# An RWKV attention and mixture-of-experts block on one core: the front's statistics, ramps, parameter loads and pieces in another order

## The chip, the cores and the metric

The kernel runs on one core of one Trainium2 chip. The metric is the device time of one execution in microseconds. Five engines work side by side: TensorE (PE in the profile, its weight loads PEld), VectorE (DVE), ScalarE (ACT), GpSimd (POOL) and SyncE (SP, which here only issues transfers). Each engine works through its own list of instructions in order. Transfers are issued by SP, ACT and POOL.

## The reference

x has 2 sequences of 2048 tokens and 256 channels, 4096 tokens in all. It is normalized twice for the attention branch, which projects three blends of each token with the token before it, runs a decaying sum over time and projects the result. The expert branch sends each token to the best two of eight experts.

```python
xn = _layernorm(x)
# attention branch: a second layer norm, with gain ln_g and bias ln_b
x2 = _layernorm(xn, ln_g, ln_b);  last = x2 shifted by one token (zero at the start)
k = (x2*mix_k + last*(1-mix_k)) @ Wk.T      # v and r likewise, with their own mix
den = den*td + exp(k);  num = num*td + exp(k)*v          # over time
attn = (sigmoid(r) * num/(den + 1e-8)) @ Wo.T
# expert branch, on xn
scores = relu(xn @ Wr + br);  the two best experts, softmax of their scores as weights
y_e = relu(xn @ W1[e] + b1[e]) @ W2[e] + b2[e]
out = x + attn + sum of weight_e * y_e
```

## The kernel before

The tokens are cut into 8 blocks of 512, and a block into 4 tiles of 128 tokens. The order of all instructions is written out by hand: the program's text is the order on each engine. The front, up to about 57 us, goes over the 8 blocks with small functions that the text calls in turn:

- load_x(b) loads a block, load_w() the next of wk, wv, wr and wo; the loop at L151 loads the six parameter vectors into the rows of one tile. SP issues the loads but for two tiles of x's block 0 and the six vectors, which ACT issues. In the compiled program a transfer of SP or ACT uses one of eight completion semaphores in turn, and waits until the transfer that had the same one before has landed.
- keep_warm(n) is n products on PE over a tile of zeros, idle, whose result nobody reads.
- stats(b): DVE takes mean and variance of each token (bn_stats, bn_aggr, L225 and L227), and POOL forms w from the variance (L230), its power of -1/2, rr (L233), for blocks 2 and 3 also mrr (L237), and ve (L238).
- normed(b): (x - mean) * rr for four tiles (L260), on DVE; in blocks 2 and 3 the first of the four on ACT (L264), with mrr. Then a store into the table that the experts gather from (L267).
- turned(b): PE transposes the block (L292), ACT writes it twice, as x2T (L295) and with the gain and bias as xaT (L305). In block 0 the first blend is made straight from the transposes (L297 on ACT, L301 on DVE), with first_by, which needs the parameter vectors: PE transposes these (colp, L488), ACT copies them to cols (L490), and DVE works unmixed and first_by out of them. x2T of block 0 is copied by DVE in turned_on() (L320).
- follow(b): POOL copies the last column of one block's xaT in front of the next's.
- mix(n): the next n of the 24 blends on DVE (L385); parts(b, i): what ACT prepares for them (L350).
- some(n): the next n of the 48 pieces of the projections. A piece is four products on PE (L415) and an evacuation by ACT (L418). From the tenth piece on each also lets ACT do one of parts.
- scored(b) and routed(b): the router's products (L330), a copy by ACT (L336) and a transpose (L341). When all eight are there, best_two() on DVE chooses the experts; divisors(h) on POOL is a power over 16 columns (L244) that it needs.

PSUM has two buffers for pieces and scores together (ps_a) and two for transposes (ps_t); blends have six, x2 three.

While pieces of later blocks run, DVE sorts the tokens by expert with tables of comparisons against the ramps lo_iota and hi_iota (L530). Then comes the expert stage, from 115 us to the end: for each unit of 128 or 256 tokens PE does the first product (L1000) and the second (L1013), weights are loaded by SP, tokens gathered and results added by POOL, and the decaying sum runs beside it on DVE.

The ramps, e_iota and other tables are written by POOL after stats(1). The memset of idle is DVE's last before the first statistics.

Of the kernel before, what the change touches and what calls it, by code (L numbers as in the profile page):

```python
# [9 lines left out]
F32 = mybir.dt.float32  # L10
BF16 = mybir.dt.bfloat16
F16 = mybir.dt.float16
# [14 lines left out]
def rwkv_moe_block(  # L27
# [42 lines left out]
    NU = K * NT + E - 1  # L70
# [38 lines left out]
    xa_pool = routing.enter_context(tc.tile_pool(name="xa", bufs=1))  # L109
    rout = routing.enter_context(tc.tile_pool(name="rout", bufs=1))  # L110
    fronts = routing.enter_context(ExitStack())
    rpool = fronts.enter_context(tc.tile_pool(name="rpool", bufs=2, side="right"))
# [36 lines left out]
        attn_w.append(t)  # L149

    for n, i in enumerate((4, 5, 1, 2, 3, 0)):  # L151
        nc.scalar.dma_start(
            rows[i * NC : (i + 1) * NC, :], vectors[i].rearrange("(c p) -> c p", p=P)
        )

# [10 lines left out]
    for b in range(4, NB):  # L166
# [4 lines left out]

    ident = const.tile([P, P], F32, name="ident")
    make_identity(nc, ident)
    power = rout.tile([P, HT], F32, name="power")
    nc.vector.memset(power, -0.5)

# [2 lines left out]
    nc.gpsimd.iota(  # L179
        place, [[NPAIR, 2]], base=0, channel_multiplier=1, allow_small_or_imprecise_dtypes=True  # L180
    )
    at_pair = rout.tile([P, 1], F32, name="at_pair")
    at_unit = place[:, 1:2]
    wlim = rout.tile([P, 2 * E], F32, name="wlim")
# [21 lines left out]

    sd2 = const.tile([P, NT], F32, name="sd2")
    sps = [ps_y.tile([P, HT, EW], F32, tag="py", name=f"sp{h}") for h in range(2)]
    rrs, mrrs, xaTs = [None] * NB, [None] * NB, [None] * NB

    def mk(nm, shape):
        return rpool.tile(shape, F32, bufs=1, name=nm)
# [3 lines left out]
    def stats(b):  # L216
        st, mv = mk(f"st_{b}", [P, NS, 6]), mk(f"mv_{b}", [P, NS, 2])
        mean, var = mv[:, :, 0], mv[:, :, 1]
        at = ts(b, NS)
        rrs[b] = rr_all[:, at]  # L220
        w, mrr = mk(f"w_{b}", [P, NS]), None

        for half in ((0, 1), (2, 3)) if b == 0 else (range(NS),):
            for i in half:
                nc.vector.bn_stats(st[:, i, :], xts[b][:, i, :])  # L225
            for i in half:
                nc.vector.bn_aggr(mv[:, i, :], st[:, i, :])  # L227
# [5 lines left out]
            nc.gpsimd.tensor_tensor(rrs[b][:, g], w[:, g], power[:, g], ALU.pow)  # L233
        if b not in NORMED:
            less_mean, mrr = mk(f"less_mean_{b}", [P, NS]), mk(f"mrr_{b}", [P, NS])
            nc.gpsimd.tensor_scalar(less_mean, mean, -1.0, 0.0, ALU.mult, ALU.add)
            nc.gpsimd.tensor_tensor(mrr, less_mean, rrs[b], ALU.mult)  # L237
        nc.gpsimd.tensor_scalar(ve_all[:, at], var, LN_EPS, 0.0, ALU.add, ALU.add)  # L238
        mrrs[b] = (mean, mrr)

    def divisors(half):

        at = slice(half * HT, (half + 1) * HT)
        nc.gpsimd.tensor_tensor(rs[:, at], ve_all[:, at], power, ALU.pow)  # L244
# [8 lines left out]
    def normed(b):  # L253
        xt = xts[b]
        mean, mrr = mrrs[b]
        x2 = x2s[b] = rpool.tile([P, NS, C], F32, tag="x2", bufs=3, name=f"x2_{b}")
        for t in range(NS):
            r = rrs[b][:, t : t + 1]
            if t or b in NORMED:
                nc.vector.tensor_scalar(  # L260
                    x2[:, t, :], xt[:, t, :], mean[:, t : t + 1], r, ALU.subtract, ALU.mult
                )
# [55 lines left out]
    def turned_on():  # L318
        for c in range(NC):
            nc.vector.tensor_copy(x2Ts[0][:, c, :], first_tps[c])  # L320
# [17 lines left out]
    def routed(b):  # L338
        i = b * NS % HT
        sp = sps[b * NS // HT][:, i : i + NS, :]  # L340
        nc.tensor.transpose(sp.rearrange("p t e -> p (t e)"), s8s[b], ident)  # L341
# [15 lines left out]
    def weighted(b, i):  # L357
        for _ in parts(b, i):
            pass
# [34 lines left out]
    def mix(n):  # L394
        for _ in range(n):
            next(blending)
# [29 lines left out]
    def some(n):  # L426
        for _ in range(n):
            next(projected)
# [41 lines left out]
        nc.vector.tensor_tensor(hot.rearrange("p e t -> p t e"), hot1, hot2, ALU.add)  # L470

    idle = rpool.tile([P, TB], BF16, bufs=1, name="idle")
    nc.vector.memset(idle, 0.0)
    warm = ps_h.tile([P, TB], F32, tag="ph", name="warm")

    def keep_warm(n):
        for _ in range(n):
            nc.tensor.matmul(warm, idle[:, 0:P], idle, start=True, stop=True)  # L480

    xaTs[0] = xa_pool.tile([P, NC, TB + 1], F32, name="xaT_0")
    nc.gpsimd.memset(xaTs[0][:, :, 0:1], 0.0)
    keep_warm(13)
    stats(0)
    normed(0)
# [7 lines left out]
    def vecs(i):  # L494
        return cols[:, i * NC : (i + 1) * NC]
# [22 lines left out]
    def count(nm, n, dtype=F32, base=0, step=1, chan=0, pool=rout):  # L518
        t = pool.tile([P, n], dtype, name=nm)
        nc.gpsimd.iota(  # L520
            t, [[step, n]], base=base, channel_multiplier=chan,
            allow_small_or_imprecise_dtypes=True,
        )
        return t

    CH = 8

    def ramp(nm, n):
        t = rout.tile([P, n, 2], F16, name=nm)
        nc.gpsimd.iota(  # L530
            t, [[1, n], [0, 2]], base=0, channel_multiplier=0,
            allow_small_or_imprecise_dtypes=True,
        )
        return t

    lo_iota, hi_iota = ramp("lo_iota", P), ramp("hi_iota", NU)
    e_iota = count("e_iota", E)

    token = rout.tile([P, NT], F16, name="token")
    for i in range(2):  # L540
        nc.gpsimd.iota(
            token[:, i * HT : (i + 1) * HT], [[P, HT]], base=(-NTOK // 2, 1)[i],
            channel_multiplier=1, allow_small_or_imprecise_dtypes=True,
# [5 lines left out]
        base=NTOK, channel_multiplier=1, allow_small_or_imprecise_dtypes=True,  # L549
# [3 lines left out]
        allow_small_or_imprecise_dtypes=True,  # L553
# [6 lines left out]
    keep_warm(2)  # L560
    some(2)
    mix(1)
    normed(1)
    turned_on()
    weighted(0, 2)
    some(2)
    turned(1)
    follow(1)
    nc.scalar.activation(td, vecs(0), AF.Exp)
    mix(1)  # L570
    scored(0)
    stats(2)
    some(2)
    routed(0)
    mix(1)
    normed(2)
    scored(1)
    some(1)
    turned(2)
    follow(2)  # L580
    stats(3)
    mix(1)
    normed(3)
    some(1)
    routed(1)
    some(1)
    scored(2)
    turned(3)
    follow(3)
    for i in range(2):  # L590
        nc.sync.dma_start(acc[NTOK + i * P : NTOK + (i + 1) * P, :], zero)
    stats(4)
    some(1)
    mix(1)
    normed(4)
    routed(2)
    some(1)
    scored(3)
    turned(4)
    follow(4)  # L600
    stats(5)
    some(1)
    routed(3)
    mix(1)
    normed(5)
    some(1)
    scored(4)
    turned(5)
    follow(5)
    stats(6)  # L610
    divisors(0)
    some(1)
    mix(1)
    normed(6)
    routed(4)
    some(1)
    scored(5)
    turned(6)
    follow(6)
    stats(7)  # L620
    divisors(1)
    some(1)
    mix(1)
    normed(7)
    routed(5)
    scored(6)
    turned(7)
    follow(7)
# [420 lines left out]
    for s in range(NSTEP):  # L1049
# [102 lines left out]
```

## Time and profile before

| | us |
|---|---|
| median of 3 runs (lowest, highest) | 654.92 (654.69, 655.28) |
| the profiled execution | 655.4 |
| its span, first to last instruction | 653.7 |
| PE busy | 635.7 (97%) |
| DVE busy | 334.7 (51%) |
| ACT busy | 230.4 (35%) |
| POOL busy | 242.0 (37%) |
| DVE busy from 20 to 50 us | 8.76, 8.97 and 8.69 of each 10 |
| ACT busy from 20 to 50 us | 6.84, 8.76 and 9.28 of each 10 |

A group of instructions is given as line, engine, operation, output<-input, sizes and count. What stands in brackets behind an instruction is how long its engine was idle just before it and what ended that. Products on PE are pipelined, so that the time from one start to the next tells more than a duration. In a table of waits the columns are the waiting engine, what it waits to do, and who released it; then the total in us, how many times, and the longest.

### The profile page before, as it was taken

How to read it: one execution, taken by the hardware profiler on the slowest of the kernel's cores; microseconds unless marked ns; L12 is line 12 of the kernel's file. 1: busy time of each engine (PE TensorE's matmuls, PEld its weight loads, DVE VectorE, ACT ScalarE, POOL GpSimd, SP SyncE). 2: the span in 40 equal slices, each digit the busy share in tenths (PEclk: the TensorE clock that was granted, in tenths of full speed). 3: DMA queues.
4: the chain of work that ended last, by engine and by line, in shares of the span. 5: the costliest groups of instructions: out<-in, count | busy, mean ns of one | idle time of the engine just before them, and what ended most of it. 6: DMA issues, size and time to landing. Idle time of an engine off the chain costs nothing. (4 is left out here: it accounts for less than half of the span.)

```text
span 653.7 us, 9070 instructions
## 1 busy us (share of the span) xinstructions
PE 635.7 (97%) x3030; PEld 496.5 (76%) x3030; DVE 334.7 (51%) x776; ACT 230.4 (35%) x474; POOL 242.0 (37%) x212
## 2 busy tenths in 40 slices
PE   7999999999999999999999999999999999999993
PEld 3454444888888888888888888888888888888882
DVE  6988997646546555757676857222211212221110
ACT  4696754342332333232323232322332222222220
POOL 3664204043243354304434373443443333343111
PEclk9999999999999999999999999999999999999997
DMA  8534505697796795789686777666667665667611
GB/s 244 199 125 163 146 0 148 244 295 204 184 315 188 189 314 182 198 274 313 185 199 178 199 204 202 185 190 178 182 193 214 211 212 173 172 181 202 194 22 17
DMA packets 92424, 124.50 MB, mean 190 GB/s; under 512 B 15468, under 2 KB 80568, under 8 KB 92248
## 3 DMA queue, kind: packets, MB, share of 16 engines
q1 hardware_dynamic: 74592, 100.77, 47.2%
q0 software_dynamic: 17472, 22.86, 18.9%
q8 instruction: 25, 0.41, 0.2%
q10 hardware_dynamic: 312, 0.27, 0.2%
q14 instruction: 23, 0.19, 0.1%
HBM read 105.89 MB, written 26.38 MB: 202 GB/s over the span
## 5 line engine op out<-in xcount | busy, mean ns | idle before, releaser
L1004 ACT ACTIVATE h<-hp,b 128x256 f32<-128x256 f32 (+1 forms) x296 | 136.2, 460 | 348.6 <-PE hp L1000 234.6
L1000 PE MATMUL hp<-xT,w 128*128 128x256 f32 (+1 forms) x1184 | 252.5, 369 | 0.9
L1013 PE MATMUL yp<-w,h 128*128 128x256 f32 x1104 | 244.4, 379 | 0.0
L1000 PEld LDWEIGHTS hp<-xT,w 128*128 128x128 f32 x1184 | 199.0, 189 | 49.8 <-ACT h L1004 18.8
L1013 PEld LDWEIGHTS yp<-w,h 128*128 128x128 f32 x1104 | 207.0, 190 | 26.6
L1025 POOL DMA_INDIRECT out_dram<-y,into x50 | 84.0, 1680 | 209.7 <-DVE y L1021 112.1
L990 DVE COPY xT<-xp 128x512 f32<-128x512 f32 (+1 forms) x37 | 24.3, 656 | 167.8 <-PE xp L988 167.8
L960 POOL DMA_INDIRECT xg<-table,frm x69 | 75.3, 1092 | 43.8 <-PE p L415 23.0
L1020 DVE TENSOR_TENSOR y<-yp,b 128x256 f32<-128x256 f32 x67 | 28.3, 423 | 105.1 <-PE yp L1013 105.1
L1025 POOL DMA_INDIRECT acc<-y,into x19 | 32.5, 1709 | 83.9 <-DVE y L1021 22.1
L898 DVE RECIPROCAL dn<-dn 128x512 f32<-128x512 f32 x16 | 53.6, 3353 | 0.5
L418 ACT ACTIVATE kvr<-p 128x512 f32<-128x512 f32 x48 | 28.7, 600 | 31.6 <-PE p L415 31.0
L415 PE MATMUL p<-mix,wk 128*128 128x512 f32 x64 | 29.8, 601 | 0.9 <-DVE mix L301 0.9
L415 PE MATMUL p<-mix,wv 128*128 128x512 f32 x64 | 29.7, 597 | 0.0
L415 PE MATMUL p<-mix,wr 128*128 128x512 f32 x64 | 29.5, 596 | 0.0
L907 PE MATMUL op<-wo,z 128*128 128x256 f32 x128 | 28.9, 379 | 0.0
L907 PEld LDWEIGHTS op<-wo,z 128*128 128x128 f32 x128 | 24.3, 190 | 3.3
L1021 DVE TENSOR_SCALAR y<-y,gate 128x256 f32<-128x256 f32 x67 | 24.6, 367 | 2.4
L385 DVE SCALAR_TENSOR_TENSOR mix<-xaT,cols,mix 128x512 f32<-128x512 f32 x34 | 24.6, 776 | 0.5 <-ACT mix L350 0.5
L350 ACT ACTIVATE mix<-xaT,unmixed 128x512 f32<-128x512 f32 x34 | 24.2, 717 | 0.0
L970 DVE TENSOR_SCALAR xg<-xg 128x256 f32<-128x256 f32 x69 | 22.7, 367 | 0.0
L415 PEld LDWEIGHTS p<-mix,wk 128*128 128x128 f32 x64 | 11.4, 190 | 13.0 <-issue 8.7
(188 smaller groups left out, 387.7 us busy)
## 6 DMA issues: line engine op xcount, KB each, us to landing
w<-in_L_ffn_W_dram SPq DMA_DIRECT2D x74, 1024.0 KB, 9.2
b<-in_L_ffn_b_dram SPq DMA_DIRECT2D x37, 128.0 KB, 4.0
table<-x SPq DMA_DIRECT2D x8, 512.0 KB, 2.9
x<-in_L_attn_x_dram SPq DMA_DIRECT2D x7, 512.0 KB, 5.8
out_dram<-o_sb POOLq DMA_DIRECT2D x5, 512.0 KB, 7.9
acc<-o_sb POOLq DMA_DIRECT2D x3, 512.0 KB, 6.2
xg<-table,frm POOLq DMA_INDIRECT x69, 6.8
out_dram<-y,into POOLq DMA_INDIRECT x50, 7.3
```

Of the source, the lines that this page charges most:

```text
L385: nc.vector.scalar_tensor_tensor(m[:, c, :], by[:, c, :], vec(1 + i, c), other[:, c, :], ALU.mult, ALU.add,)
L415: nc.tensor.matmul(p, w[:, c, ts(o, P)], m[:, c, :], start=(c == 0), stop=(c == NC - 1))
L418: nc.scalar.activation(kvr[b][:, i, o, :], p, f, scale=sign)
L898: nc.vector.reciprocal(dn, dn)
L907: nc.tensor.matmul(op, z[:, c, ts(t, P)], wo_sb[:, c, :], start=(c == 0), stop=(c == NC - 1))
L960: nc.gpsimd.indirect_dma_start(out=g, out_offset=None, in_=table, in_offset=bass.IndirectOffsetOnAxis(ap=frm[:, u : u + 1], axis=0), bound ...
L1000: nc.tensor.matmul(hp, w1_sb[:, c, ts(j, P)], xT[:, c, :], start=(c == 0), stop=(c == NC - 1))
L1004: nc.scalar.activation(h[:, 0:n], hp, AF.Relu, bias=b1_sb[:, j : j + 1])
L1013: nc.tensor.matmul(yp, hs[j][:, ts(i, P)], w2_sb[:, j, :], start=(j == 0), stop=(j == NH - 1))
L1020: nc.vector.tensor_tensor(y, yp, b2_sb, ALU.add)
L1021: nc.vector.tensor_scalar(y, y, gates[s][i], None, ALU.mult)
L1025: return nc.gpsimd.indirect_dma_start(out=to, out_offset=bass.IndirectOffsetOnAxis(ap=into[:, u : u + 1], axis=0), in_=y, in_offset=None, ...
```

## The change

- The parameter vectors: the first three (gain, bias, mix_k) are still issued by ACT, the other three (mix_v, mix_r, time_decay) by SP, behind x's block 0 and in front of wk.
- The memset of idle moves from the end of DVE's memsets to behind the first of them. The memset of xaT's first column goes in front of the ramp place on POOL.
- lo_iota and hi_iota move from behind stats(1) to POOL's very beginning, before stats(0). e_iota stays; a helper with one use left is written out.
- turned_on() now stands ahead of normed(1).
- stats(b) moves up from block 2 on: stats(2) comes directly behind turned(1), and each stats(b+1) is called before normed(b). divisors follow stats(6) and stats(7) as before.
- Pieces, blends, scores and transposes are called in another order: from block 2 on a turned comes directly behind the score of the block before it, and two pieces follow, where before one stood on each side.

The changed kernel has the same operations as before; only their order, and the queue of three small transfers, differ.

```diff
     for n, i in enumerate((4, 5, 1, 2, 3, 0)):
-        nc.scalar.dma_start(
+        (nc.scalar if n < 3 else nc.sync).dma_start(
             rows[i * NC : (i + 1) * NC, :], vectors[i].rearrange("(c p) -> c p", p=P)
         )
...
     ident = const.tile([P, P], F32, name="ident")
     make_identity(nc, ident)
+
+    idle = rpool.tile([P, TB], BF16, bufs=1, name="idle")
+    nc.vector.memset(idle, 0.0)
+    xaTs = [None] * NB
+    xaTs[0] = xa_pool.tile([P, NC, TB + 1], F32, name="xaT_0")
+    nc.gpsimd.memset(xaTs[0][:, :, 0:1], 0.0)
     power = rout.tile([P, HT], F32, name="power")
     nc.vector.memset(power, -0.5)
...
+    CH = 8
+
+    def ramp(nm, n):
+        t = rout.tile([P, n, 2], F16, name=nm)
+        nc.gpsimd.iota(
+            t, [[1, n], [0, 2]], base=0, channel_multiplier=0,
+            allow_small_or_imprecise_dtypes=True,
+        )
+        return t
+
+    lo_iota, hi_iota = ramp("lo_iota", P), ramp("hi_iota", NU)
...
-    idle = rpool.tile([P, TB], BF16, bufs=1, name="idle")
-    nc.vector.memset(idle, 0.0)
     warm = ps_h.tile([P, TB], F32, tag="ph", name="warm")
...
-    xaTs[0] = xa_pool.tile([P, NC, TB + 1], F32, name="xaT_0")
-    nc.gpsimd.memset(xaTs[0][:, :, 0:1], 0.0)
     keep_warm(13)
     stats(0)
     normed(0)
...
-    lo_iota, hi_iota = ramp("lo_iota", P), ramp("hi_iota", NU)
-    e_iota = count("e_iota", E)
+    e_iota = rout.tile([P, E], F32, name="e_iota")
+    nc.gpsimd.iota(
+        e_iota, [[1, E]], base=0, channel_multiplier=0, allow_small_or_imprecise_dtypes=True
+    )
...
     keep_warm(2)
     some(2)
     mix(1)
+    turned_on()
     normed(1)
-    turned_on()
     weighted(0, 2)
     some(2)
     turned(1)
     follow(1)
     nc.scalar.activation(td, vecs(0), AF.Exp)
+    stats(2)
     mix(1)
     scored(0)
-    stats(2)
     some(2)
     routed(0)
-    mix(1)
+    stats(3)
     normed(2)
     scored(1)
-    some(1)
+    mix(1)
     turned(2)
     follow(2)
-    stats(3)
+    some(1)
+    stats(4)
+    normed(3)
+    some(1)
+    routed(1)
     mix(1)
-    normed(3)
-    some(1)
-    routed(1)
-    some(1)
     scored(2)
     turned(3)
     follow(3)
+    some(1)
+    stats(5)
...
-    stats(6)
-    divisors(0)
-    some(1)
-    mix(1)
+    some(1)
+    stats(7)
+    some(1)
+    divisors(1)
     normed(6)
     routed(4)
-    some(1)
+    mix(1)
     scored(5)
     turned(6)
     follow(6)
-    stats(7)
-    divisors(1)
-    some(1)
-    mix(1)
+    some(1)
     normed(7)
     routed(5)
+    some(1)
+    mix(1)
     scored(6)
     turned(7)
     follow(7)
```

More of the change, by code (lines that the diff above doesn't have):

```diff
@@ L208, in rwkv_moe_block @@
     sps = [ps_y.tile([P, HT, EW], F32, tag="py", name=f"sp{h}") for h in range(2)]
-    rrs, mrrs, xaTs = [None] * NB, [None] * NB, [None] * NB
+    rrs, mrrs = [None] * NB, [None] * NB
     def mk(nm, shape):
@@ L517, in rwkv_moe_block @@
     )
[L518 to L534, printed above, removed]
-    lo_iota, hi_iota = ramp("lo_iota", P), ramp("hi_iota", NU)
-    e_iota = count("e_iota", E)
+    e_iota = rout.tile([P, E], F32, name="e_iota")
+    nc.gpsimd.iota(
+        e_iota, [[1, E]], base=0, channel_multiplier=0, allow_small_or_imprecise_dtypes=True
+    )
     token = rout.tile([P, NT], F16, name="token")
@@ L589, in rwkv_moe_block @@
     follow(3)
+    some(1)
+    stats(5)
     for i in range(2):
         nc.sync.dma_start(acc[NTOK + i * P : NTOK + (i + 1) * P, :], zero)
-    stats(4)
     some(1)
-    mix(1)
     normed(4)
     routed(2)
-    some(1)
+    mix(1)
     scored(3)
@@ L600, in rwkv_moe_block @@
     follow(4)
-    stats(5)
     some(1)
+    stats(6)
+    divisors(0)
+    some(1)
+    normed(5)
     routed(3)
     mix(1)
-    normed(5)
-    some(1)
     scored(4)
@@ L609, in rwkv_moe_block @@
     follow(5)
-    stats(6)
-    divisors(0)
     some(1)
-    mix(1)
+    stats(7)
+    some(1)
+    divisors(1)
     normed(6)
     routed(4)
-    some(1)
+    mix(1)
     scored(5)
@@ L619, in rwkv_moe_block @@
     follow(6)
-    stats(7)
-    divisors(1)
+    some(1)
+    normed(7)
+    routed(5)
     some(1)
     mix(1)
-    normed(7)
-    routed(5)
     scored(6)
```

## The prediction

> **What bounds the kernel now.** I read, in this order, the page's shares and slices, the timeline of TensorE (PE), the waits of VectorE (DVE) and of PE in the first 60 us, and the timelines of DVE, GpSimd (POOL), ScalarE (ACT) and SP there. PE is busy for 97% of the span, and its expert stage hardly waits: the line group of L1000 has 0.9 us of idle time in all. The chain of waits breaks off at the last scatter, so I follow PE itself. All edits act before about 57 us; what they give is how much earlier PE gets through this front.
>
> ```profile
> span 653.7 us, 9070 instructions
> PE 635.7 (97%) x3030; PEld 496.5 (76%) x3030; DVE 334.7 (51%) x776; ACT 230.4 (35%) x474; POOL 242.0 (37%) x212
> ```
> ```profile
> 2.68 5.73 PE L480 MATMUL warm<-idle 128*128 128x512 bf16 x13 [2.68 <-DVE idle L475]
> 8.34 0.23 PE L488 MATMUL colp<-ident,rows 12*128 12x12 f32 x1
> ...
> 10.91 3.70 PE L415 MATMUL p<-mix,wk 128*128 128x512 f32 x8 [0.89 <-DVE mix L301]
> 14.45 3.60 PE L415 MATMUL p<-mix,wv 128*128 128x512 f32 x8
> 18.65 1.22 PE L292 MATMUL tp<-ident,x 128*128 128x128 f32 x8 [0.61 <-DVE x2T L320]
> ...
> 50.22 0.64 PE L330 MATMUL p<-x2T,wr_sb 128*32 128x128 f32 x16
> 51.35 1.64 PE L292 MATMUL tp<-ident,x 128*128 128x128 f32 x8 [0.49 <-DVE x L260]
> 52.83 1.88 PE L415 MATMUL p<-mix,wr 128*128 128x512 f32 x4
> ...
> 55.84 0.33 PE L341 MATMUL sp<-ident,s 128*128 128x128 f32 x1 [0.44 <-ACT s L336]
> ...
> 57.82 0.27 PE L635 MATMUL b1p<-ident,b_rows 64*128 64x64 f32 x1
> ```
> Columns: start, duration, engine. From start to next start a piece (four products) costs 1.72 us, a block's transposes 0.93, a score 0.57, a routing 0.11. From 10.91 to 57.82 PE does 18 pieces, 7 transposes, 8 scores, 8 routings: 30.96 + 6.51 + 4.56 + 0.88 = 42.9 us of work in 46.9. So 4.0 us are lost, about 1.0 of it in 0.1 us steps when PE changes from one kind to another.
>
> ```profile
> DVE x L260 <- POOL rr_all L233: 5.8, 8, 1.2
> ```
> ```profile
> 15.34 2.57 DVE L260 TENSOR_SCALAR x<-x,mv,rr_all 128x256 f32<-128x256 f32 x4 [0.93 <-POOL rr_all L233]
> 17.83 1.27 DVE L320 COPY x2T<-tp 128x512 f32<-128x512 f32 x2
> ...
> 45.33 1.39 DVE L260 TENSOR_SCALAR x<-x,mv,rr_all 128x256 f32<-128x256 f32 x4 [0.92 <-POOL rr_all L233]
> ```
> ```profile
> 16.24 1.52 POOL L530 IOTA lo_iota<- 128x256 f16 x1
> 17.73 0.88 POOL L530 IOTA hi_iota<- 128x142 f16 x1
> ...
> 45.58 2.95 POOL L244 TENSOR_TENSOR rs<-ve_all,power 128x16 f32<-128x16 f32 x1
> ```
> DVE stands still eight times before the normalization, waiting for POOL's power of the variance. Once the four L260 take 2.57 instead of 1.39 us: the fourth starts at 16.34 and takes 1.57, until lo_iota is over.
>
> **The change, part by part.** Durations are those of the one profiled execution: span 653.7, with 1.7 around it 655.4, 0.5 over the median of 654.92. Differences found in it are taken off the median.
>
> *Warm-up.* The memset of idle moves in front of the other 13 on DVE: done at about 1.2 instead of 2.62, so warm starts at 1.25 instead of 2.68. Its 13 products follow each other by 0.427 us (5.55), so they end at 6.8 instead of 8.2. The memsets behind it end as before; DVE's wait for x until 3.82 (1.2 us) covers them.
>
> *Parameter rows.* ACT issues three (0.54, 0.24, 0.24), SP the other three, ahead of wk. In the compiled order each transfer waits until the eighth before it has landed. The last row now goes out when x's first tile has landed, by 3.82, not at 4.54. The trace has no landing time for rows: at most 3.8 us (from 4.54 to colp's weight load at 8.33), and in the nearest row, x's first tiles on this queue, 3.1. So colp can run between 6.9 and 7.6. Shorter than 3.1 gains nothing, as warm ends at 6.8. From colp to ACT's first L297 (8.34 to 9.29) are 0.95 us. L297 also needs normed(0), on DVE until 7.71 as before, its transposes, and 0.5 us of small DVE operations behind it: 8.15 at the earliest. So L297 starts between 8.15 and 8.55 and gains 1.14 to 0.74; I take 1.0, nearer the row of the same queue. The first piece starts at 9.9.
>
> *What the rows delay.* wk waits for x's fourth tile, x_1 for its third, landed by 4.44: they go out at about 4.3 and 4.7, not 1.76 and 2.24. wk took 4.9 us to land (x_2 waited for it until 6.64), so 9.2 against 9.9 where it is needed. x_1 took 5.8, at most 6.2 for any block: 10.9 against 10.44, where DVE first reads it; a 512 KB write into table took 2.9, which gives 7.6. I take zero: PE needs mix1_0 only 0.67 us after DVE has it and mix2_0 0.42 after, so up to 0.4 us late is free; beyond that it costs one for one. Later blocks are read 5 us or more after they land.
>
> *Ramps.* lo_iota and hi_iota (2.4 us) run on POOL from 1.64 to 4.1, where it sat idle until 4.88 for DVE's mv: nothing, with 0.7 to spare, then one for one on normed(0). They leave 16.24.
>
> *Block 1.* turned_on's two copies (1.19) now fill the 0.93 wait ahead of normed(1), and L260 is not held. DVE: bn and aggregates 10.44 to 12.03, mix 13.33, copies 14.52, normed(1) 15.82; before that was 19.02 with the copies. PE's transposes no longer wait: from 14.45 to 19.80 it took 5.35, it needs 3.44 + 0.93 + 0.1, which gives 0.88. stats(2) now stands before mix2_0, whose first half is there at 18.15, PE wanting it at 18.57.
>
> *Statistics a block ahead.* POOL's chain for the next block (0.6 + 1.41 and 0.55) runs beside another block's normalization, and the 5.8 us of waits go. On PE this removes what they caused: 1.13 and 1.48 from 50.22 to 52.83 instead of 0.57 and 0.93 (1.11), and the piece at 29.29, behind ACT's wait for mrr, 2.07 instead of 1.72 (0.35). In return the next block's statistics (1.60) stand before each normed on DVE: normed(2) ends at 21.3, 1.6 before PE can turn it, normed(7) near 43, six before. If that cover went, it would be one for one on turned.
>
> *Pieces dealt anew.* turned(2) follows scored(1) directly, one piece sooner, and a new wait appears: its first quarter is ACT's L264, queued behind the evacuation of wr's second piece. PE ends wr at 22.1, routes and scores until 22.88; ACT evacuates 22.3 to 22.8 and has L264 at 23.4. Behind L264 wait x2T and xaT of block 2, with PE. Bounds 0 (were L264 earlier) and 0.7 (were it queued for the whole 0.6 and 0.1); I take 0.58. From block 3 to block 6 both orders pace 5.15 us per block (0.93 + 2 × 1.72 + 0.11 + 0.57 + 0.1). The wait of routed(7) for s (0.5) stays.
>
> Sum: 1.0 + 0.88 + 1.11 + 0.35 − 0.58 = 2.76, call it 2.7. routed(7) ends near 53.5. What is late next? From 57.82 PE does six pieces until the count of the experts at 68.42; its input hot was ready at 64.45, and moves 3.2 earlier as DVE no longer works up to 56.81: covered. From 68.84 to 98.99 DVE is the bound, started by this count, so all moves together; the weight loads follow DVE's choice of experts. 654.92 − 2.7 = 652.2.
>
> **Rivals.**
> (a) *The front does not start earlier.* The rows still land with the old end of warm-up, or PE's clock opens later. The 13 warm products run at 0.427, the two at 9.42 at about half that. With warm ending at 6.8 PE idles 0.8 us, and the clock may stay slow into the first pieces. The gain is then 1.7: 653.2. The Trainium skill (TensorE: Matmul & The Clock Gate, section "Part 1: The HAM clock gate") says that a free-running window of 3.4 us has to be busy; by that rule the release could slip to about 11.5 and cost an estimated 0.8; the trace's 13 slow products agree, the phase of the window is not shown.
> (b) *New waits eat the reorder*: ACT, busy 9.3 of 10 us from 40 to 50, is late again at each turned. With only the front and 0.2 left the gain is 1.2: 653.7. Against it: ACT's work for a block is 2.26 + 0.15 + 1.0 + 1.22 = 4.6 of 5.15.
> (c) *Slower: POOL's power holds DVE.* normed(b) now runs beside the power of block b+1 (1.0 to 1.41 us), as the fourth L260 was held by lo_iota. Six normed would be held: 6.0 to 8.5 us. DVE's own work from 9.1 is 39.9 us, so it ends at 49.0, 4.2 before the score needs it at 53.2; the rest, 1.8 to 4.3, comes off the gain: 653.1 to 656.5. It is slower than before from 1.15 us per block. For it: lo_iota. Against it: the power of 45.58 took 2.95 us, and L260 beside it took its usual 1.39. The Trainium skill (SBUF — State Buffer, section "Who interferes with whom") speaks for this rival: a VectorE tensor_scalar and a GpSimd instruction share a port pair, and the second blocks until the first ends. lo_iota agrees with it, the power at 45.58 does not, and I go by the latter.
> (d) *Nothing arrives at the end*: a transfer that doesn't move sets the expert stage. 654.9. Against it: PE's 0.9 us there.
> (e) *x_1 lands later than 6.2 us after its issue.* At 8 us 1.8 is lost: 654.0.
>
> **How the numbers follow.** As worked out 0.62; (a) 0.16; (b) 0.09; (c) 0.06; (d) 0.03; (e) 0.04. Predicted 652.2. The bounds of the terms give 651.5 to 652.9 for it, with another 0.2 below for run and profile. Up to 653.7 (a) and most of (b) are in; what is left out is some 0.15. About 0.2%, 1.3 us, is what a measurement can tell from no change. Faster by more: 0.62 + 0.16 + half of (b) + 0.01 = 0.83. Slower by more: 0.05, from (c) above all and a long (e). The rest, 0.12, is within.
>
> **What would show it.** In the profile after: warm starting near 1.25, colp by 7.6, the first piece near 9.9; lo_iota over by 4.2; no wait of DVE for rr_all behind block 0; L260 at 1.3 to 1.4 for four beside every power; a PE wait of about 0.6 ahead of turned(2); b1p near 55.1 and the count near 65.7. It would be wrong if the first piece stays near 10.9, if a product waits for a transfer of wk or x, if normed takes over 2 us, or if the expert stage shows waits for weights.

## The result

| | before | after |
|---|---|---|
| median, same chip (lowest, highest) | 655.28 (654.69, 656.31), 5 runs | 651.80 (651.56, 651.85), 5 runs |
| the profiled execution, its span | 655.4, 653.7 | 651.85, 650.1 |
| first piece of the projections on PE | 10.91 | 9.65 |
| b1p, a transposition of the experts' biases: the end of the front | 57.82 | 54.81 |
| first product of the expert stage | 114.87 | 111.87 |
| from there to the end of the span | 538.8 | 538.2 |

The changed kernel takes 0.9945 of the time before, with a 95% interval of 0.993 to 0.996. It is faster by 3.5 us between the medians, against a forecast of 2.7 from 654.92, the median of the first three of the five runs before; 652.2 was forecast, 651.80 came. The last four lines of the table, from one profiled execution of each kernel, say where it is from: 1.26 us up to the first piece, 1.75 between the first piece and b1p, nothing between b1p and the first product (57.05 and 57.06), and 0.6 behind that.

The page of the changed kernel, its span and its shares:

```profile
span 650.1 us, 9068 instructions
PE 634.3 (98%) x3030; PEld 496.6 (76%) x3030; DVE 333.2 (51%) x776; ACT 230.2 (35%) x474; POOL 238.1 (37%) x212
```

PE is busy for 1.4 us less than before (634.3 for 635.7), in a span 3.6 shorter: 2.2 of the 3.6 is idle time that went. The rest is busy time that holds short waits: the transposes of block 7 took 1.64 and take 1.09, the first products of the expert stage together 252.5 and 251.9. The timeline of PE in the changed kernel (start, duration, engine, line; L494 is the warm-up, L432 a piece, L309 transposes, L347 a score, L358 a routing):

```profile
1.30 5.73 PE L494 MATMUL warm<-idle 128*128 128x512 bf16 x13 [1.30 <-DVE wlim L202]
6.96 0.26 PE L500 MATMUL colp<-ident,rows 12*128 12x12 f32 x1
...
9.65 3.70 PE L432 MATMUL p<-mix,wk 128*128 128x512 f32 x8 [0.84 <-DVE mix L318]
13.18 3.60 PE L432 MATMUL p<-mix,wv 128*128 128x512 f32 x8
16.62 1.04 PE L309 MATMUL tp<-ident,x 128*128 128x128 f32 x8
...
22.05 0.64 PE L347 MATMUL p<-x2T,wr_sb 128*32 128x128 f32 x16
23.18 1.09 PE L309 MATMUL tp<-ident,x 128*128 128x128 f32 x8 [0.49 <-ACT x L281]
...
48.32 0.64 PE L347 MATMUL p<-x2T,wr_sb 128*32 128x128 f32 x16
48.90 1.09 PE L309 MATMUL tp<-ident,x 128*128 128x128 f32 x8
...
52.83 0.33 PE L358 MATMUL sp<-ident,s 128*128 128x128 f32 x1 [0.44 <-ACT s L353]
...
54.81 0.27 PE L631 MATMUL b1p<-ident,b_rows 64*128 64x64 f32 x1
```

The transposes of block 1 (16.62) and of block 7 (48.90) now follow what stands before them without a wait. The transposes of block 2 (23.18) have a wait that was not there, 0.49 us for the quarter of normed(2) that ACT does; with the step from one kind of work to the next the score takes 1.13 there and not 0.57. The routing of block 7 still waits for ACT.

DVE's waits in the first 60 us of the changed kernel (who waits, for whom; total, times, longest):

```profile
DVE score L473 <- PE sp L358: 3.4, 1, 3.4
...
DVE x L277 <- POOL rr_all L250: 0.6, 2, 0.3
```

The eight waits for POOL's power, 5.8 us, have come down to the two of block 0. DVE is now early by 3.4 us at the end of the front (it waits there for the routing of block 7), where PE had waited 0.49 us for it ahead of block 7's transposes.

The ramps on POOL in the changed kernel, and on DVE the normalization of block 1, which they had held:

```profile
1.58 1.51 POOL L192 IOTA lo_iota<- 128x256 f16 x1
3.06 0.88 POOL L192 IOTA hi_iota<- 128x142 f16 x1
4.72 0.19 POOL L247 TENSOR_SCALAR w<-mv 128x2 f32<-128x2 f32 x1 [0.78 <-DVE mv L244]
```
```profile
14.26 1.54 DVE L277 TENSOR_SCALAR x<-x,mv,rr_all 128x256 f32<-128x256 f32 x4
```

They are over at 3.94, 0.78 before POOL has work, and the four normalizations take 1.54, where before they took 2.57.

### The profile page after: what moved, and what is told of

Same layout as the page of the kernel before. It is cut to its first block, busy times and chain, and to the rows that moved or that the text cites. A ratio compares the mean times of both kernels' runs of the same rounds, so it can differ in the third digit from the quotient of the medians.

```text
span 650.1 us, 9068 instructions
## 1 busy us (share of the span) xinstructions
PE 634.3 (98%) x3030; PEld 496.6 (76%) x3030; DVE 333.2 (51%) x776; ACT 230.2 (35%) x474; POOL 238.1 (37%) x212
## 5 line engine op out<-in xcount | busy, mean ns | idle before, releaser
L996 PE MATMUL hp<-xT,w 128*128 128x256 f32 (+1 forms) x1184 | 251.9, 369 | 0.8
L1021 POOL DMA_INDIRECT out_dram<-y,into x50 | 82.2, 1644 | 214.9 <-DVE y L1017 127.8
L1021 POOL DMA_INDIRECT acc<-y,into x19 | 30.6, 1608 | 85.0 <-issue 26.5
L432 PE MATMUL p<-mix,wk 128*128 128x512 f32 x64 | 29.4, 599 | 0.8 <-DVE mix L318 0.8
L432 PE MATMUL p<-mix,wv 128*128 128x512 f32 x64 | 29.5, 597 | 0.0
L432 PE MATMUL p<-mix,wr 128*128 128x512 f32 x64 | 29.5, 598 | 0.0
L432 PEld LDWEIGHTS p<-mix,wk 128*128 128x128 f32 x64 | 11.5, 190 | 13.3 <-issue 9.6
```

Source lines behind the costliest of these rows:

```text
L432: nc.tensor.matmul(p, w[:, c, ts(o, P)], m[:, c, :], start=(c == 0), stop=(c == NC - 1))
L996: nc.tensor.matmul(hp, w1_sb[:, c, ts(j, P)], xT[:, c, :], start=(c == 0), stop=(c == NC - 1))
L1021: return nc.gpsimd.indirect_dma_start(out=to, out_offset=bass.IndirectOffsetOnAxis(ap=into[:, u : u + 1], axis=0), in_=y, in_offset=None, ...
```

## The experiments

Each undoes or adds one thing; v_best and v_pre stand on v_normed. "Interior" is the time from the first piece to b1p on PE. All columns but the median are from one profiled execution. Chips differ a little, so the kernel before is given on the same chip. Its own runs spread by 1.5 us or more on each chip, so the 95% interval of a ratio reaches 0.6 to 1 us to each side: by these intervals only o_order (0.9985 to 1.0003) and v_pre (0.9902 to 0.9928) are clear of the changed kernel (0.993 to 0.996). What the other edits do is read from their traces.

| | median (before, same chip) | first piece | interior | first product | to the end |
|---|---|---|---|---|---|
| before | 655.28 | 10.91 | 46.91 | 114.87 | 538.8 |
| after | 651.80 (655.28) | 9.65 | 45.16 | 111.87 | 538.2 |
| u_warm: idle's memset last | 652.63 (655.73) | 10.91 | 45.16 | 113.12 | 538.2 |
| u_rows: six rows on ACT | 653.90 (655.73) | 11.28 | 45.17 | 113.50 | 538.9 |
| u_ramps: ramps behind stats(1) | 653.15 (655.73) | 9.65 | 46.51 | 113.20 | 538.2 |
| u_order: the old order of calls | 652.78 (655.73) | 9.61 | 45.80 | 112.45 | 538.2 |
| warm6: 6 products of warm-up | 653.41 (655.72) | 9.80 | 46.58 | 113.41 | 538.3 |
| x1_late: x_1 behind all weights | 653.05 (655.72) | 9.79 | 46.82 | 113.64 | 538.3 |
| v_normed: no quarter on ACT | 651.93 (655.72) | 9.86 | 44.73 | 111.60 | 538.8 |
| v_best: and a piece moved | 651.99 (655.72) | 9.70 | 44.55 | 111.52 | 538.8 |
| rows_behind: rows behind wk, x_1 | 652.49 (655.35) | 10.64 | 45.17 | 112.85 | 538.3 |
| o_order: before, new order alone | 654.90 (655.35) | 11.07 | 46.52 | 114.63 | 538.8 |
| v_pre: no quarter, count earlier | 649.77 (655.35) | 9.64 | 44.75 | 109.94 | 538.0 |
| base: the changed kernel again | 651.89 (655.35) | 9.74 | 45.17 | 111.97 | 538.2 |

**u_warm.** The memset of idle goes back to the end of DVE's memsets.

```diff
-    idle = rpool.tile([P, TB], BF16, bufs=1, name="idle")
-    nc.vector.memset(idle, 0.0)
     xaTs = [None] * NB
...
+    idle = rpool.tile([P, TB], BF16, bufs=1, name="idle")
+    nc.vector.memset(idle, 0.0)
     warm = ps_h.tile([P, TB], F32, tag="ph", name="warm")
```

> The changed kernel, but with idle's memset as DVE's last again. My theory: warm starts at 2.7, colp runs at 8.3, the first piece starts at 10.8 to 10.9, all 1.1 to 1.25 later than in the changed kernel, and so does b1p (near 56): 652.9 to 653.1. The rival, that the rows' earlier landing carries the front's gain: colp and the first piece stay near 7 and 9.7, 651.8.

PE in this kernel:

```profile
2.68 5.72 PE L494 MATMUL warm<-idle 128*128 128x512 bf16 x13 [2.68 <-DVE idle L489]
8.34 0.23 PE L500 MATMUL colp<-ident,rows 12*128 12x12 f32 x1
...
10.91 3.70 PE L430 MATMUL p<-mix,wk 128*128 128x512 f32 x8 [0.89 <-DVE mix L316]
```

The warm-up starts at 2.68 again, colp at 8.34, the first piece at 10.91, 1.26 later than in the changed kernel, and the interior keeps its 45.16. The whole gain of the front is lost in this execution, although the rows go out on two queues. The times show less of it: 3.1 us below the kernel before on the same chip, where the changed kernel is 3.5 below, with one of the four runs at 651.88. The thirteen products do not always take 5.72 us; in u_rows they took 4.29. With that length the warm-up would be over at 7.0 here, by estimate, and hold nothing. Whether that is what the shorter runs did, no trace shows.

**u_rows.** All six parameter rows on ACT, as before.

```diff
     for n, i in enumerate((4, 5, 1, 2, 3, 0)):
-        (nc.scalar if n < 3 else nc.sync).dma_start(
+        nc.scalar.dma_start(
```

> The changed kernel, but with all six parameter rows issued by ACT again. My theory: colp waits for the end of the 13 warm products in both kernels (its weight load comes 0.98 us after the last of theirs in both traces), so the rows' move gives little: colp stays at 6.95, the first piece at 9.65, b1p at 54.8, the time at 651.8 within 0.3; wk and x_1 go out 2 us sooner and nothing uses it. The rival, that the rows bind as soon as the warm-up ends early: the last row goes out near 4.4 and lands up to 3.3 us later, colp runs near 7.5 to 7.7, the first piece 0.3 to 0.6 later, 652.1 to 652.4.

The front was worse than the kernel before, and the first of the two theories fell. PE in this kernel:

```profile
1.29 4.29 PE L494 MATMUL warm<-idle 128*128 128x512 bf16 x13 [1.29 <-DVE wlim L202]
8.74 0.20 PE L500 MATMUL colp<-ident,rows 12*128 12x12 f32 x1 [3.15 <-DMA rows<-n_L_attn_time_decay_dram]
...
11.28 3.70 PE L432 MATMUL p<-mix,wk 128*128 128x512 f32 x8 [0.89 <-DVE mix L318]
```

The last row went out on ACT at 4.40 and PE could use it at 8.74, 4.3 us later. In the kernel before the end of the warm-up, 8.2, had hidden this. So in these traces an earlier warm-up alone gives nothing, and earlier rows alone give nothing (u_warm): the two limits lay about 0.5 us apart, and only both edits together move the first piece. Which of the two came last in the old start was a matter of the warm-up's length: in o_order, with that start and a warm-up of 5.17 us, the rows hold colp for 0.68. The times of u_rows also scatter more than those of the others (652.81 to 656.62 in ten runs). Its two longest, 656.17 and 656.62, had a mean granted clock of 0.989 and 0.990, the other eight 0.993 to 0.996; no trace of these two shows what lowered it.

**rows_behind.** Why were those rows late: ACT's queue, or what was under way ahead of them? Here the three rows stay on SP, but wk and x's block 1 go out first.

```diff
     for n, i in enumerate((4, 5, 1, 2, 3, 0)):
+        if n == 3:
+            load_w()
+            load_x(1)
         (nc.scalar if n < 3 else nc.sync).dma_start(
...
-    for b in (1, 2, 3):
+    for b in (2, 3):
```

> The changed kernel, with its last three parameter rows on SP as there, but behind wk and x's block 1 and not ahead of them. It asks why six rows on ACT were late: there the last row went out at 4.40 and had landed 4.3 us later, with wk and x_1 under way since 1.76 and 2.24; in the changed kernel with a short warm-up it went out at 3.66 on SP, ahead of wk, and had landed 1.7 us later. Theory one, a small row behind bulk transfers lands late, whatever its queue: wk and x_1 go out near 1.8 and 2.3, the last row near 4.4 or 4.6, colp waits for it until 8.4 to 9.0, the first piece starts between 10.9 and 11.5, b1p is 1.3 to 1.9 later than 54.81, the time 653.0 to 653.8. Theory two, it was ACT's queue: the last row lands 1.7 us after its issue, at 6.1 to 6.4, warm-up covers it, the first piece stays at 9.6 to 9.9 and the time within 0.3 us of the changed kernel.

The issues of SP in this kernel (SPq is SP's sequencer), and then its PE:

```profile
1.75 0.44 SPq L148 DMA_DIRECT2D wk<-in_L_attn_Wk_dram  x1
2.23 0.47 SPq L122 DMA_DIRECT2D x<-in_L_attn_x_dram  x1
...
4.39 0.25 SPq L155 DMA_DIRECT2D rows<-n_L_attn_time_decay_dram  x1
```
```profile
8.10 0.20 PE L503 MATMUL colp<-ident,rows 12*128 12x12 f32 x1 [1.07 <-DMA wv<-in_L_attn_Wv_dram]
```

From the issue of the last row to colp 3.7 us pass, on SP's queue, with 1.07 us of waiting ahead of colp. The line names a transfer of wv, but colp reads only ident and rows, and ident had been there since 1.5; so the rows are taken to be what it waited for. Theory one holds in kind, and its size was a little smaller (first piece at 10.64, not 10.9 to 11.5; the time 652.49, not 653.0 to 653.8). ACT's queue was not the reason: on either queue a row behind wk and x_1 was late.

**warm6.** Six idle products, not thirteen.

```diff
-    keep_warm(13)
+    keep_warm(6)
```

> The changed kernel with 6 idle products in place of 13. At 0.427 us each they end near 3.9, not 6.8, so PE reaches colp when the last parameter row has landed, which is not seen in the changed kernel (there colp runs at 6.96, behind the warm-up). The theory that the clock is what the warm-up buys: with 3 us of idle time ahead of the first pieces these run at the slow clock, 0.43 us a product in place of 0.21 to 0.23, until it opens again; the first two pieces of wk take 7 in place of 3.5 us if that holds through them, b1p is 1 to 4 us later, and the time 653 to 656. The rival: the few products around 8 us and the pieces open it at once or it is not lost, colp runs at 6.5 to 6.9, the first blend waits for normed(0) and its transposes as before, and the time stays within 0.4 us of the changed kernel.

```profile
1.30 2.74 PE L494 MATMUL warm<-idle 128*128 128x512 bf16 x6 [1.30 <-DVE wlim L202]
5.33 0.25 PE L500 MATMUL colp<-ident,rows 12*128 12x12 f32 x1 [1.29 <-DMA rows<-n_L_attn_time_decay_dram]
...
8.74 1.06 PE L494 MATMUL warm<-idle 128*128 128x512 bf16 x2
9.80 5.11 PE L432 MATMUL p<-mix,wk 128*128 128x512 f32 x8
```

Two answers in one timeline of PE. First, the last row, issued on SP at 3.66 ahead of wk, had landed at 5.33: 1.7 us, against 3.7 and 4.3 us behind bulk transfers. Second, the clock theory holds: the two products at 8.74 take 1.06 where the changed kernel's take 0.59, the first two pieces 5.11 and not 3.70, and the interior grows by the same 1.4 us. Against the kernel before on the same chip the time is 2.3 us lower, where the changed kernel's is 3.5 lower.

**x1_late.** The three weights go out in a row, then x's blocks.

```diff
-    for b in (1, 2, 3):
-        load_w()
-        load_x(b)
+    load_w()
+    load_w()
+    load_w()
+    for b in (1, 2, 3):
+        load_x(b)
```

> The changed kernel with wk, wv and wr issued in a row and then x's blocks 1, 2 and 3, where the changed kernel alternates them. x's block 1 goes out at 4.52 there; behind two weights more it goes out 1.0 to 1.6 us later. The theory of the forecast: it has been landing up to 5.8 us after its issue, DVE first reads it at 10.2, so it comes at about 11.4 to 11.9; stats(1) and with it the blends of block 0 that DVE has behind it are 1 to 1.7 us late, of which 0.4 is free, so 0.6 to 1.3 us come one for one on the end: 652.4 to 653.1. The rival: it lands in 3 to 4 us, as a transfer of that size can when less is in flight, DVE reads it without a wait, and the time stays within 0.3 us of the changed kernel.

DVE in this kernel:

```profile
12.18 1.40 DVE L244 BATCH_NORM_STATS2 st<-x 128x6 f32<-128x256 f32 x4 [1.79 <-DMA x<-in_L_attn_x_dram]
13.51 0.36 DVE L246 BATCH_NORM_AGGREGATE mv<-st 128x2 f32<-128x6 f32 x4
13.79 1.38 DVE L404 SCALAR_TENSOR_TENSOR mix<-xaT,cols,mix 128x512 f32<-128x512 f32 x2
```

x_1 was issued at 5.65 and read at 12.18, 6.5 us later; in the changed kernel, issued at 4.52, it was there within 5.7. DVE waits 1.79, the blends of block 0 stand behind that wait, and the interior is 1.65 longer than base's. The theory holds, at a higher price than I gave it: at most 0.15 of the wait was free, not 0.4. In the changed kernel the same read (at 10.18) waits for nothing.

**u_ramps.** The ramps behind stats(1) again.

```diff
-    lo_iota, hi_iota = ramp("lo_iota", P), ramp("hi_iota", NU)
...
+    lo_iota, hi_iota = ramp("lo_iota", P), ramp("hi_iota", NU)
     e_iota = rout.tile([P, E], F32, name="e_iota")
```

> The changed kernel, but with lo_iota and hi_iota behind stats(1) again. My theory: lo_iota now starts near 14.9, while normed(1) runs from 14.26, and holds one of its four for about 1.2 us; normed(1) ends near 17 and not 15.7, turned(1) waits up to 0.4, and mix0_2 behind stats(2) comes 0.8 late for wr: b1p 0.6 to 1.0 later, 652.4 to 652.8. The rival, that the slack of the new order hides it: b1p at 54.8, 651.8.

The normalization of block 1 on DVE, then POOL beside it, both in this kernel:

```profile
14.27 3.10 DVE L276 TENSOR_SCALAR x<-x,mv,rr_all 128x256 f32<-128x256 f32 x4
```
```profile
14.85 1.52 POOL L192 IOTA lo_iota<- 128x256 f16 x1
16.34 0.88 POOL L192 IOTA hi_iota<- 128x142 f16 x1
```

The four L276 take 3.10; in the changed kernel the same four take 1.54. All else behind them on DVE is late by as much: the transposes of block 1 wait after three of eight (16.62 to 17.42), and the first piece for wr starts at 19.69, not 18.16. The interior is 1.35 longer, more than the 0.6 to 1.0 expected.

**u_order.** The new start (warm-up, rows, ramps), but the calls in the order of the kernel before: normed(1) ahead of turned_on, stats behind the blends, one piece on each side of a turned. The core of it:

```diff
-    turned_on()
     normed(1)
+    turned_on()
...
-    stats(2)
     mix(1)
     scored(0)
+    stats(2)
...
-    some(1)
-    stats(4)
+    stats(3)
+    mix(1)
     normed(3)
...
```

> The kernel before with the warm-up, the rows and the ramps changed, but with its own order of statistics, pieces and blends. My theory: the first piece starts at 9.65 as in the changed kernel, and the waits that the new order removes are back, 1.13 and 1.48 around turned(7) for 0.57 and 0.93 and a piece of 2.07 for 1.72, less the new wait of 0.56 at turned(2): b1p 0.9 later than in the changed kernel, near 55.7, 652.7. The rival, that an earlier front and free DVE let the old order catch up: b1p within 0.3 of 54.8, 651.8 to 652.1.

DVE's waits in its first 60 us, and PE's timeline:

```profile
DVE x L277 <- POOL rr_all L250: 5.5, 7, 1.2
```
```profile
16.58 1.04 PE L309 MATMUL tp<-ident,x 128*128 128x128 f32 x8
...
47.86 0.64 PE L347 MATMUL p<-x2T,wr_sb 128*32 128x128 f32 x16
48.94 1.64 PE L309 MATMUL tp<-ident,x 128*128 128x128 f32 x8 [0.44 <-DVE x L277]
50.42 1.88 PE L432 MATMUL p<-mix,wr 128*128 128x512 f32 x4
```

With the old order DVE waits 5.5 us for the power again, where the changed kernel has 0.6, and PE loses 0.64 in all. The order is worth no more than that, net of the wait for ACT that it brings; b1p is at 55.41, between the theory's 55.7 and the rival's 55.1. The transposes of block 1 do not wait here (16.58), although turned_on stands behind normed(1): what freed them was the ramps.

**o_order.** The other way round: the kernel before with the new order alone.

```diff
-    normed(1)
     turned_on()
+    normed(1)
...
+    stats(2)
     mix(1)
     scored(0)
-    stats(2)
...
```

> The kernel before with the new order of statistics, pieces and turned_on alone: warm-up, rows and ramps as before. The theory that the parts add up: against the changed kernel it lacks the front (1.26, as undoing the warm-up cost) and the ramps (1.35, as putting them back cost), so b1p is at 54.81 + 1.26 + 1.35 = 57.4, 0.4 earlier than before, and the time 0.4 below it, no difference that the times can show. The rival: the terms of the forecast stand by themselves, 1.11 + 0.35 - 0.58 and part of the 0.88, so that the order alone gives 0.9 to 1.7 us and b1p is at 56.1 to 56.9.

PE in this kernel:

```profile
8.53 0.20 PE L488 MATMUL colp<-ident,rows 12*128 12x12 f32 x1 [0.68 <-DMA rows<-n_L_attn_time_decay_dram]
```

b1p is at 57.59 (57.4 expected), with an interior of 46.52, 0.39 less than before, and a ratio of 0.9994 with an interval of 0.9985 to 1.0003. The first piece is at 11.07, 0.16 later than before, because the rows hold colp here. The parts add up, and without the earlier ramps the order gives 0.39 on PE: normed(1) is held by the ramps as before.

**v_normed.** No quarter on ACT.

```diff
-    NORMED = (0, 1, 4, 5, 6, 7)
+    NORMED = tuple(range(NB))
```

> The changed kernel, but with all of normed(2) and normed(3) on DVE: no quarter on ACT (L281), no mrr. In the changed kernel PE goes from the score of block 1 at 22.05 to turned(2) at 23.18, 1.13 us where a score costs 0.57, and the wait in front of turned(2), 0.49 us, ends with ACT's quarter. The theory of the term of 0.58: the quarter, queued on ACT behind an evacuation, is the whole of it. Then turned(2) starts 0.56 us earlier, the first transposition of the experts' biases (b1p) moves from 54.81 to about 54.25, and the time is about 651.2, 0.6 below the changed kernel; DVE takes 0.34 us more for each of the two blocks, which its 3.4 us of idle time in front of the scores cover. The rival: x2T's or xaT's copies on ACT or the tenth piece are late there in any case, the wait only changes its releaser, and b1p stays within 0.15 us of 54.81.

```profile
22.26 0.64 PE L347 MATMUL p<-x2T,wr_sb 128*32 128x128 f32 x16
22.83 1.09 PE L309 MATMUL tp<-ident,x 128*128 128x128 f32 x8
```

The wait is gone, from the score to the transposes it is 0.57, and the interior is 0.43 shorter. b1p is at 54.59, not 54.25: the first piece was 0.1 to 0.2 later than in the two profiles of the changed kernel, for x's first tile landed later (DVE's first statistics at 3.87, not 3.66 and 3.75). The stretch behind the first product was 0.6 longer. The time, 651.93, is 3.8 us below the kernel before on its chip, where the changed kernel is 3.5 below, with intervals that overlap almost wholly. The term is confirmed by the trace; as a gain in the time it is not shown.

**v_best.** In addition the last piece ahead of b1p goes in front of routed(7).

```diff
     scored(7)
-    routed(7)
     some(1)
+    routed(7)
```

> The same without the quarter on ACT, and also the last piece ahead of b1p moved in front of routed(7), so that PE has work while ACT copies the scores of block 7 (a wait of 0.44 us in the changed kernel, and 1.08 us from that score to the routing where 0.57 is usual). The theory that every wait of PE in the front comes one for one off the end: b1p near 53.75 and the time near 650.7, 1.1 us below the changed kernel. The rival: the routing, now one piece (1.72 us) later, starts best_two on DVE about 0.7 us later, and the count of the experts and the tables behind it are late by it; then the first product of the expert stage moves by 0.6 us at most, whatever b1p does. For the theory: the experts' masks are ready at 60.6 in the changed kernel and PE counts them at 65.42, 4.8 us later.

PE, and then DVE, in this kernel:

```profile
52.23 1.98 PE L432 MATMUL p<-mix,wr 128*128 128x512 f32 x4 [0.21 <-ACT kvr L435]
54.05 0.27 PE L358 MATMUL sp<-ident,s 128*128 128x128 f32 x1
...
80.30 0.44 PE L835 MATMUL inv<-oh_t,oh_a 128*128 128x71 f16 x8 [1.32 <-DVE oh_t L827]
```
```profile
54.36 0.29 DVE L473 TENSOR_TENSOR score<-sp,sd 128x128 f32<-128x128 f32 x1 [4.59 <-PE sp L358]
```

A wait of 0.44 became one of 0.21, for ACT's evacuation, and the interior is 0.18 shorter than v_normed's. But the routing is later, DVE stands 4.59 us for it, and PE waits 1.32 for DVE at 80.30, where in v_normed it waits 1.07. b1p comes at 54.25, not 53.75, and counted from the first piece the first product is 0.08 later than v_normed's. The rival's price holds, its way there only in part: the count on PE is not late (64.86 for 65.20). DVE works without a gap from the routing to the scan behind the count, since the two waits for ACT that it had in v_normed (0.30 and 0.97) take up the late start. At this place DVE's chain is the bound, not PE.

**v_pre.** That pointed to another place. Here, without the quarter on ACT, the count of the experts (pre) stands two pieces earlier on PE, and one blend later on DVE.

```diff
-    some(6)
+    some(4)
     pre = ps_t.tile([P, 2, E * NT], F32, tag="pt", name="pre")
...
-    mix(3)
+    some(2)
+    mix(2)
     some(4)
     cum = rt("cum", (P, E, NT))
...
+    mix(1)
     some(1)
     pos = rt("pos", (P, E, NT), tag="cand")
```

> The changed kernel without the quarter on ACT, and with the count of the experts two pieces (3.4 us) earlier on PE, the first of two halves of a blend later on DVE: the scan then starts when the count is there, with no DVE wait for ACT's part of that blend in front of it (0.29 and 0.96 us in the changed kernel). The theory that behind the front DVE's chain is the bound: the count is at about 61.8, the scan near 63, DVE stands 1.2 us less, PE's wait of 1.1 us for oh_t at 80.63 goes, the first product comes at 110.4 to 110.9 (111.87 in the changed kernel), and the time is 650.4 to 650.9. The rival: DVE is busy all the same, the blend put off makes PE wait for it near 72, and the first product stays within 0.4 us of 111.5.

```profile
61.56 0.27 PE L648 MATMUL pre<-hot,upper 128*128 128x256 bf16 x1
...
78.94 0.45 PE L837 MATMUL inv<-oh_t,oh_a 128*128 128x71 f16 x8
...
109.94 4.26 PE L998 MATMUL hp<-xT,w 128*128 128x256 f32 x19
```

The count is at 61.56 (65.52 in base), PE's wait ahead of inv is gone, the first product is 2.03 earlier than base's and 0.5 earlier than the theory had it. The time is 649.77 (649.61 to 649.89), 0.9915 of the kernel before, with an interval of 0.9902 to 0.9928, and 2.1 below base on the same chip. It beats both kernels, and the 650.4 to 650.9 that was expected. The earlier count and the blend put off were not tried one without the other, and why the gain is larger than expected is open.

**base.** The changed kernel once more, to have it on the chip of these runs.

> The changed kernel itself, on the chip of these runs: 651.8 as before, first piece at 9.6 to 9.9, b1p at 54.8, first product at 111.9; from there to the end 538.2 us or, as in the kernel before and in three of the experiments, 538.8.

651.89 (651.82 to 651.93): ratio 0.9947, interval 0.9935 to 0.996, as the first time.

## Why the prediction was right

**The front, forecast 1.0, measured 1.26.** Two reasons. x's first tile landed 0.16 earlier in the profiled execution (DVE's first statistics at 3.66 and not 3.82), which the change has no part in. And the landing time of the rows was taken from the wrong row: 3.1 us, by x's first tiles, where a small row ahead of the bulk takes 1.7 (warm6). So colp never waited for it; it ran at the end of the warm-up, the lower bound. What then sets the first piece is the other limit that the forecast gave, normed(0) and its transposes, with the first blend at 8.15 at the earliest: it came at 8.03. In base colp ran at 5.95 and the first piece still started at 9.74. The term was mis-sized by taking a middle where the lower bound held; the earlier landing of x is luck.

**What the rows delay, forecast zero.** Right: DVE reads x_1 at 10.18 without a wait. x1_late shows that the concern, rival (e), was real: 1.79 us late costs 1.65.

**Ramps and block 1, forecast 0.88.** Right in size (from the pieces for wv to the score of block 0 PE takes 4.40 where it took 5.35, 0.95 less), but part of the cause was wrong. The forecast gave it to the ramps and to turned_on together. u_order has only the ramps of the two, and its transposes of block 1 already come 6.97 us after the first piece, as in the changed kernel, where before it was 7.74.

**Statistics a block ahead, forecast 1.11 + 0.35.** The 1.11 at block 7 is there: u_order has these waits (1.08 and 1.48 between starts), the changed kernel has 0.58 and 0.93. The 0.35 belongs elsewhere: the piece that took 2.07 takes 1.81 in u_order, with the statistics in their old place. So 0.26 of it came from the ramps too. In sum the ramps gave 1.11 (46.91 to 45.80), the order 0.64 (to 45.16). Forecast by the same cut they were 0.88 and 0.88; the errors cancel, 1.75 against 1.76, and that is luck: the sum came out, the split did not. The two also depend on each other: with the new order the ramps give 1.35 (u_ramps), and without the earlier ramps the order gives 0.39 (o_order).

**The new wait at turned(2), forecast −0.58.** Measured 1.13 for 0.57: −0.56, for the reason given. v_normed takes it away.

**Behind b1p everything moved together**, as forecast: b1p −3.01, count −3.00, first product −3.00. The profiled executions differ by 0.6 more, 538.8 against 538.2 from the first product to the end. That stretch was 538.0 to 538.3 in nine of the fourteen profiles and 538.8 to 538.9 in five, with changed kernels in both groups (u_rows, v_normed and v_best in the second), and PE's idle time at the first product's line is 0.8 to 0.9 in all of them. The 0.6 lies in the first products' busy time: 251.7 to 251.9 us in the nine, 252.5 in the five. Between the changed kernel and v_normed it is two steps of about 0.27 us; at the second one a weight load of PE waits 0.43 us for ACT's evacuation h, where in the changed kernel it waits 0.15. Why ACT is late there is open, and the forecast had nothing for it. Between medians, 3.5 us may hold 3.0 from the front and some 0.5 of this; which of the runs without a profile had it is not shown.

**The rivals.** (a), in the form that rows hold the front back, is what u_rows shows: it was the fate of the warm-up without the rows' new place. In its other form, the clock, it did not come: the first two pieces took 3.70 us, as before. warm6 shows its price, 1.4 us on the first pieces, where the forecast had put an estimated 0.8. (b) stayed at the one wait. (c), POOL's power holds DVE, fell. (Its range was also summed wrongly: with 1.8 to 4.3 us off the gain, 652.2 becomes 654.0 to 656.5, not 653.1 to 656.5.) DVE's normalizations of blocks 5 and 6 in the changed kernel, and the power on POOL beside each:

```profile
33.39 1.38 DVE L277 TENSOR_SCALAR x<-x,mv,rr_all 128x256 f32<-128x256 f32 x4
...
38.92 1.38 DVE L277 TENSOR_SCALAR x<-x,mv,rr_all 128x256 f32<-128x256 f32 x4
```
```profile
33.93 1.08 POOL L250 TENSOR_TENSOR rr_all<-w,power 128x4 f32<-128x4 f32 x1
...
39.47 1.05 POOL L250 TENSOR_TENSOR rr_all<-w,power 128x4 f32<-128x4 f32 x1
40.61 1.39 POOL L255 TENSOR_SCALAR ve_all<-mv 128x4 f32<-128x4 f32 x1
```

Four in 1.38 us, beside a power of 1.05 to 1.08. If one is held it is POOL: its small ve took 0.24 at 14.13 and takes 1.39 here, beside DVE's blends. The Trainium skill (SBUF — State Buffer, section "Who interferes with whom") says that VectorE with two inputs from SBUF gets in the way of a GpSimd instruction that reads there; the blends have two such inputs, and this agrees. (d) did not come, the front's gain arrived in full.

## What to carry to other kernels

An edit that lifts one of two limits that lie close together shows nothing by itself: the warm-up and the parameter rows had to move together, and in the traces undoing either lost the whole 1.26 us or more. Small loads that the first work needs are best sent out ahead of the bulk ones. And idle time of an engine that is not the bound is a poor measure of a gain: taking away 4.9 us of DVE's waits gave 0.64 on PE, while moving the count on PE, small products in front of DVE's long chain, with a blend put off behind it, gave some 1.5 (the first product 2.03 earlier, less 0.42 for the quarter and 0.10 for the start).

## What was unexpected in the hardware

- A small row took 1.7 us from issue to use with little under way, and 3.7 and 4.3 us behind a weight and a block of x, on SP's queue (rows_behind) and on ACT's (u_rows).
- The thirteen products of warm-up took 5.72 or 5.73 us in five profiles and 4.29 to 5.63 in the other eight that have thirteen. At 0.427 us for a slow product and half of it for a fast one (0.21 between the last starts of u_rows), 4.29 us (u_rows) means an estimated six slow ones: the clock opened some 2.7 us after the first, where in the changed kernel's profile all thirteen were slow. The Trainium skill (TensorE: Matmul & The Clock Gate, section "Part 1: The HAM clock gate") says that the number of slow products differs from run to run, as its window runs freely; the traces agree: the same kernel's took 5.73 us in one profile and 4.72 in another (base). With the new start it did not move the first piece (9.65 and 9.74).
- In u_rows PE idled 3.15 us behind the warm-up and its first two pieces still took 3.70, at the fast clock. In warm6, with six products of 2.74 us, they took 5.11.
- An iota of 1.52 us on POOL, with one of 0.88 behind it, held four normalizations on DVE by 1.56 (3.10 for 1.54); a power of 1.05 us held them not at all (1.38).
